# Second products of a dense mixture-of-experts stage turned round: channels on partitions, the gates spread as rows by DMA

## The chip, the core and the metric

The kernel runs on one core of a Trainium2 chip. The metric is device time in microseconds (us) of one execution. Three runs of the kernel before gave 791.85, 794.53 and 795.11 us, a median of 794.53 us. One further execution was recorded by the hardware profiler.

## What is computed

The input is 8 sequences of 256 tokens with 128 channels. The program is a chain of residual blocks: a feed-forward block, an attention block and a feed-forward block with the weights of layer 0, and then the same three of layer 1. The change concerns the two feed-forward blocks of layer 1, here called **f0** (before the attention of layer 1) and **f1** (after it, the last block of the program). Cut to what matters:

```python
def _L1_ffn_ref(x, Wg, W1, W2):           # 2048 tokens, 128 channels, F = 256, E = 8
    probs = softmax(xt @ Wg)
    _, top_idx = top_k(probs.T, T // E)   # every expert takes its 256 best tokens
    masked = where(sel, pT, -inf)
    tok2exp = where(assigned, argmax(masked), argmax(pT))      # one expert per token
    weights = take(probs, tok2exp)
    for e in range(E):
        gate = where(tok2exp == e, weights, 0.0)
        h = gelu(xt @ W1[e]) @ W2[e]
        out = out + gate[:, None] * h
x = x + 0.5 * _L1_ffn_ref(layernorm(x), ...)
x = x + attention(x)
x = x + 0.5 * _L1_ffn_ref(layernorm(x), ...)
```

Which expert a token belongs to is known only when all tokens have been counted for all experts. Each token then needs one expert.

## The kernel before, in words

The tokens lie in 16 tiles of 128. In f0 and f1 the 16 tiles form four groups of four tiles (512 tokens). Two of the groups are **sorted**: their tokens are scattered by expert into a buffer in DRAM (`scattering`, POOL), fetched again as tiles of one expert each (`fetching`, tiles `xs`), turned on PE (`ptpf`), multiplied with the weights of that one expert (`experts`: `phpf`, `pypf`), stored, and gathered back by token (`returning`, POOL, tiles `ygf`). This can begin only after the choice. The other two groups are **dense** (`everyone`): every one of the 8 experts is computed for all their tokens, and what a token doesn't need is multiplied by a gate of zero. This can begin before the choice, and fills PE while the choice is made. Sixteen such units (2 groups by 8 experts) are computed in each block.

A unit of `everyone` has two first products `phf` (line 1652: a 128x128 block of W1 is stationary, the 512 tokens move), two activations `hf` on ACT, and second products `pyf` (line 1670). Before the change a second product keeps 128 tokens of `hf` stationary and moves the 128 columns of W2, so that tokens lie on partitions in the result; a unit has four tiles by two halves of F, eight products. The profile shows every product of 32-bit numbers as two matmul instructions (two passes), so a unit has sixteen `pyf` and four `phf` instructions.

`settling` takes the result. If the gates aren't known yet, ACT copies it out of its bank of PSUM (line 1702: the first eight into `W2`, whose contents are no longer needed, the rest into tiles with the tag `w`). Once the gates are known, DVE adds each of the four tiles with one `scalar_tensor_tensor` (line 1707), with the gate as a value per partition. When eight experts are in, the tile is marked as `moved`. The attention of a sequence waits for both of its tiles; in f0, sequences 0 to 3 lie in the dense groups and 4 to 7 in the sorted ones. The stores of the output wait for the tiles of f1.

The choice (`choosing`) is a search for a threshold in ten rounds. In each round DVE makes candidates and compares (`L1547`, two halves), PE counts with ones (`pcf`, line 1541, eight matmuls a half), and DVE takes the counts and moves the threshold (`L1559`, `L1563`). Then PE ranks ties (`pkf`, line 1575), DVE picks one expert per token, PE counts places (`pcrf`, lines 546 to 571), and DVE computes slots and the gates (line 1620).

No engine chooses its own order. A planner in the kernel (`Weave`) runs all these generators against assumed durations, such as `yield "pe", 1.0, 0.2`, and writes the instructions of each engine down in the order in which its own clock meets them. Each engine then executes its list in that order. A stream of rank -1 (`everyone`) gives way to others that are ready at the same planned time. So an assumed duration decides how many dense products stand between two counts in the list of PE. SP issues the transfers from one list in the same way: the weights of the sorted experts (line 683), the tiles `xs` (line 819), the results of the experts (line 857) and the outputs (line 1750). PSUM has two banks for results of second products (`y`), and a unit that isn't copied holds its bank until DVE has read it.

Of the kernel before, what the change touches and what calls it, by code (L numbers as in the profile page):

```python
# [9 lines left out]
F32 = mybir.dt.float32  # L10
# [3 lines left out]
ALU = mybir.AluOpType  # L14
# [4 lines left out]
P = 128  # L19
B, S, D = 8, 256, 128  # L20
NH, HD = 16, 8
E = 8
SL = P // B
NT = S // SL
TB = 4
# [12 lines left out]
QSCALE = 1.0 / HD**0.5  # L38


LAGS = {"pe": 0.5, "act": 0.3, "dve": 0.2, "pool": 0.2, "sp": 2.5}


# [66 lines left out]
def kernel(ctx: ExitStack, tc: tile.TileContext, a: dict, out: bass.AP):  # L110
# [66 lines left out]
    def bank(tag, k, shape, name):  # L177

        return psum["pool"].tile(shape, F32, tag=f"{tag}{k % BANKS[tag]}", name=name, bufs=1)
# [9 lines left out]
    def woven(dram, moe, pools):  # L189
# [521 lines left out]
        def second1(e, f):  # L711

            cols = slice(F1 + f * D, F1 + (f + 1) * D)
            if isinstance(e, int):
                return l1["W"][:, e, cols]
            return l1["W"][:, bass.ds(e, 1), cols].rearrange("p e d -> p (e d)")
# [786 lines left out]
        def choosing(key):  # L1503
# [125 lines left out]
            c["mine"] = mine  # L1629
            mark(("mine", key))  # L1630

        def everyone(key):

            n_f = F1 // P
            before = None

            yield ("through", unsorted[-1]) if key == "f0" else ("weights of", 4 * B - 1)
            c = chosen[key]
            order = [(k, e) for k in ALL[key] for e in range(E)]
            for n, (k, e) in enumerate(order + [(None, None)]):  # L1640
                hs = []
                if e == 0:
                    yield "head", key, k
                if before:
                    yb = yield from acquire("y")
                    py = bank("y", yb, [P, TB, D], f"py{key}_{n}")
                for f in range(n_f):
                    if k is not None:
                        hb = yield from acquire("h")
                        yield "pe", 1.0, 0.2  # L1650
                        ph = bank("h", hb, [P, BW], f"ph{key}_{n}_{f}")
                        pe.matmul(  # L1652
                            ph, lhsT=l1["W"][:, e, f * P : (f + 1) * P], rhs=c["xT"][k], start=True,
                            stop=True,
                        )
                        h = hidden(f"h{key}_{n}_{f}")

                        def gelu(h=h, ph=ph):
                            act.activation(h, ph, AF.Gelu)  # L1659

                        weave.spawn(emptying(hb, 0.6, gelu, GELU))
                        hs.append((h, hb))
                    if before:

                        for i in range(f * TB // n_f, (f + 1) * TB // n_f):
                            for b in before[1]:
                                yield "free", "h", b
                            yield "pe", 0.5, 0.2
                            for ff in range(n_f):
                                pe.matmul(  # L1670
                                    py[:, i, :], lhsT=before[0][ff][:, i * P : (i + 1) * P],
                                    rhs=second1(before[3], ff), start=ff == 0, stop=ff == n_f - 1,
                                )
                if before:
                    weave.spawn(settling(key, py, yb, before[2], before[3], n), 3 if ("gate", key) in weave.done else None)
                if e == E - 1:
                    mark(("through", (key, k)))
                before = [h for h, _ in hs], [b for _, b in hs], k, e


        SHARED = 12

        added = {}
        kept = dict.fromkeys(("f0", "f1"), 0)

        def settling(key, py, yb, k, e, n):

            c = chosen[key]
            src = py
            waits = ("gate", key) not in weave.done  # L1690
            if waits:
                i = kept[key]
                kept[key] += 1
                if key == "f1" and i >= E:
                    yield "weighed", 4 * B - 1
                yield "act", 0.57, 0.15
                if i < E:

                    src = W2[:, i, :].rearrange("p (t d) -> p t d", d=D)
                else:  # L1700
                    src = one([P, TB, D], f"y{key}_{n}", "w", SHARED)
                act.copy(src, py)
                mark(("free", "y", yb))
            yield "gate", key
            for i, t in enumerate(GROUPS[key][k]):
                yield "dve", 0.28, 0.0
                dve.scalar_tensor_tensor(  # L1707
                    x1[:, t, :], src[:, i, :], c["gate"][:, t, e : e + 1], x1[:, t, :], ALU.mult, ALU.add
                )
            if not waits:  # L1710
                mark(("free", "y", yb))
            added[key, k] = added.get((key, k), 0) + 1
            if added[key, k] == E:
                for t in GROUPS[key][k]:
                    mark(("moved", key, t))

        def returning(key):

# [125 lines left out]
        def scoring():  # L1844
            for n in range(4 * B):
                b, j = divmod(n, 4)
                if j == 0:
                    yield "projected", b
                if n == 0:
                    for t in GROUPS["f0"][ALL["f0"][1]]:  # L1850
                        yield "moved", "f0", t
                if n > 2:
                    yield "weighed", n - 3
                q, k, _, _ = made[b]
                pss = yield from s_banks([([P, 2, S], f"ps{b}_{j}_{g}") for g in range(4)])
                yield "pe", 1.05, 0.2
                for kc in range(2):
                    for g in range(4):
                        rows = slice(32 * g, 32 * g + 32)
                        pe.matmul(  # L1860
                            pss[g][0][:, kc, :], lhsT=k[rows, j, kc * P : (kc + 1) * P],
                            rhs=q[rows, :], start=True, stop=True,
                        )
                ws = [one([P, 2, S], f"w{b}_{j}_{g}", "w", SHARED) for g in range(4)]
                relued[n] = ws
                left = [4]
                for g in range(4):
                    weave.spawn(relu_of(n, g, *pss[g], ws[g], left))
# [50 lines left out]
        def attended(b, sums):  # L1919
# [33 lines left out]
            for qc in range(2):  # L1953
# [17 lines left out]
            [  # L1971
                (1, loading()), (1, fetching()), (1, routing()), (1, tensor()), (2, adds()), (2, combines()),
                (0, scanning()), (3, preparing()), (2, constants()), (2, finishing()), (2, moving()), (1, clearing()),
                (1, opening()), (3, heads("f0")), (-1, everyone("f0")), (1, experts("f0")), (2, returning("f0")),
                (3, projecting()), (1, scoring()), (2, weighing()),
                (3, heads("f1")), (-1, everyone("f1")), (1, experts("f1")), (2, returning("f1")), (1, storing()),
            ]
        )

# [70 lines left out]
```

## Time and profile before

| | |
|---|---|
| three runs | 791.85, 794.53, 795.11 us |
| profiled execution, its own time | 793.47 us |
| its span in the trace | 791.7 us |
| PE busy | 694.4 us (88%) |
| weight loads of PE (beside it) | 568.0 us (72%) |
| DVE busy | 520.2 us (66%) |
| ACT busy | 414.7 us (52%) |
| POOL busy | 214.2 us (27%) |

The stretches that matter, read off the timelines of the engines (us from the start of the span):

| | f0 | f1 |
|---|---|---|
| first dense product on PE | 469.50 | 678.78 |
| first count | 491.95 | 696.57 |
| ranking of ties on PE | 518.46 | 722.53 |
| first scatter on POOL | 529.08 | 733.56 |
| SP begins the weights of the sorted experts | 530.02 | 734.49 |
| SP begins the tiles `xs` | 540.78 | 745.90 |
| first sorted tile turned on PE | 545.08 | 748.98 |
| next stage | attention's first scores 564.64 | first gather on POOL 776.41 |

A line of the timeline gives the start, the time from the first start to the last end of equal instructions merged (xN), the engine, the line of the kernel, the operation, and the tiles out and in. What stands in brackets is idle time of that engine before it and what ended it. Ends of matmuls are modelled, so the distance between starts says more than the duration. Buffer numbers are left out of the names: `f` stands for f0 and f1 alike.

### The profile page before, as it was taken

What the parts mean: (1) busy time and instruction counts of PE and PEld (TensorE: products, weight loads), DVE (VectorE), ACT (ScalarE), POOL (GpSimd) and SP (SyncE); (2) the same over time, 40 slices, a digit from 0 to 9 for tenths busy, and PEclk for the clock granted to TensorE, in tenths of its full rate; (3) what the DMA queues carried; (4) which work ended last, traced back from release to release, by engine and by line L of the source; (5) the groups of instructions that cost most, each with busy time, mean ns of one, the idle gap of its engine ahead of it and who ended that gap; (6) DMA issues with size and microseconds to landing.
All of it is one profiled execution on the core that took longest, in us unless ns stands there. A gap on an engine that the chain in (4) does not pass through costs nothing.

```text
span 791.7 us, 17430 instructions
## 1 busy us (share of the span) xinstructions
PE 694.4 (88%) x5538; PEld 568.0 (72%) x5538; DVE 520.2 (66%) x2946; ACT 414.7 (52%) x1002; POOL 214.2 (27%) x327
## 2 busy tenths in 40 slices
PE   5999999978798659878989998998999999999990
PEld 3889998966596449658979886676756565677690
DVE  2545489788998899889712314768377677475811
ACT  4464866833787417624547545333656656543340
POOL 2234530037114310170351301022144242300403
PEclk9999999985899569958979999999999999999996
DMA  9163876615535265455487200014110000000512
GB/s 333 35 210 91 241 223 173 169 48 180 144 97 117 49 200 161 107 174 150 128 251 223 79 12 28 2 42 136 41 39 1 2 2 1 2 1 1 184 47 77
DMA packets 104570, 83.09 MB, mean 105 GB/s; under 512 B 40544, under 2 KB 83808, under 8 KB 104480
## 3 DMA queue, kind: packets, MB, share of 16 engines
q1 hardware_dynamic: 99568, 71.59, 31.1%
q0 software_dynamic: 4480, 9.18, 3.7%
q10 hardware_dynamic: 432, 1.20, 0.4%
q8 instruction: 46, 0.75, 0.4%
q14 instruction: 44, 0.36, 0.2%
HBM read 57.94 MB, written 24.00 MB: 104 GB/s over the span
## 4 chain that ended last, share of the span: by engine, by line
PE 60%; DVE 24%; DMA 5%; POOL 4%; issue 3%; ACT 3%; SPq 0%; POOLq 0%; ACTq 0%; DVEq 0%
PE phpout L898 6%; PE pypout L875 5%; PE ps L1860 5%; PE pa L1904 4%; PE pyf L1670 3%; PE pmo L1297 3%; PE phdin L769 3%; PE pydin L779 3%; PE phpin L898 2%; PE phf L1652 2%; DVE x L1707 2%; DVE r L1265 2%; DVE mk L1234 2%; PE pypin L875 2%; DVE u L1256 2%
## 5 line engine op out<-in xcount | busy, mean ns | idle before, releaser
L1670 PEld LDWEIGHTS pyf<-w_W,hf 128*128 128x128 f32 x512 | 68.1, 193 | 19.0 <-issue 18.6
L902 ACT ACTIVATE hpout<-phpout,w 128x128 f32<-128x128 f32 x224 | 63.9, 369 | 28.8 <-PE phpout L898 24.2
L1670 PE MATMUL pyf<-w_W,hf 128*128 128x128 f32 x512 | 76.0, 282 | 0.0
L1659 ACT ACTIVATE hf<-phf 128x512 f32<-128x512 f32 x64 | 38.1, 597 | 67.3 <-PE phf L1652 67.2
L1652 PE MATMUL phf<-xTf,w_W 128*128 128x512 f32 x128 | 66.8, 606 | 0.0
L898 PE MATMUL phpout<-xTpout,w 128*128 128x128 f32 x448 | 62.9, 287 | 1.4 <-ACT xTpout L848 1.4
L898 PEld LDWEIGHTS phpout<-xTpout,w 128*128 128x128 f32 x448 | 57.7, 202 | 3.4 <-ACT xTpout L848 2.0
L875 PE MATMUL pypout<-W,hpout 128*128 x448 | 59.7, 277 | 0.0
L1265 DVE SCALAR_TENSOR_TENSOR r<-kbs,dot,e 128x8 f32<-128x8 f32 x251 | 56.2, 224 | 0.0
L1234 DVE TENSOR_TENSOR mk<-Ms,kns 128x72 f32<-128x72 f32 x251 | 55.5, 221 | 0.0
L1256 DVE TENSOR_TENSOR u<-kbs,r 128x64 f32<-128x64 f32 x256 | 55.3, 216 | 0.1
L902 ACT ACTIVATE hpin<-phpin,w 128x128 f32<-128x128 f32 x160 | 45.3, 374 | 19.0 <-PE phpin L898 12.1
L1297 PE MATMUL pmo<-qmo,ident 128*128 128x128 f32 x256 | 43.0, 337 | 14.0 <-DVE qmo L1291 12.5
L875 PEld LDWEIGHTS pypout<-W,hpout 128*128 128x128 f32 x448 | 54.8, 193 | 0.1
L1876 DVE TENSOR_SCALAR w<-ps 128x512 f32<-128x512 f32 x64 | 42.6, 684 | 17.6 <-PE ps L1860 17.0
L1261 DVE TENSOR_TENSOR Ms<-Ms,u 128x64 f32<-128x64 f32 x251 | 53.9, 215 | 0.0
L1229 DVE TENSOR_REDUCE e<-mk 128x8 f32<-128x72 f32 x251 | 53.8, 214 | 0.0
L1297 PEld LDWEIGHTS pmo<-qmo,ident 128*128 128x128 f32 x256 | 40.2, 247 | 16.7 <-DVE qmo L1291 14.4
L1873 ACT ACTIVATE w<-ps 128x512 f32<-128x512 f32 x64 | 36.2, 597 | 25.8 <-PE ps L1860 25.7
L898 PE MATMUL phpin<-xTpin,w 128*128 128x128 f32 x320 | 44.0, 283 | 1.7 <-ACT sps L1049 0.9
L1860 PE MATMUL ps<-q,k 32*128 32x256 f32 x512 | 43.1, 403 | 2.3 <-ACT w L1873 1.3
L898 PEld LDWEIGHTS phpin<-xTpin,w 128*128 128x128 f32 x320 | 40.5, 199 | 3.5 <-ACT sps L1049 1.6
(382 smaller groups left out, 1606.4 us busy)
## 6 DMA issues: line engine op xcount, KB each, us to landing
w<-in_w_dram SPq DMA_DIRECT2D x112, 258.0 KB, 3.4
xs<-rows SPq DMA_DIRECT2D x27, 256.0 KB, 4.2
rows<-x SPq DMA_DIRECT2D x5, 768.0 KB, 5.2
w<-in_w_dram SPq DMA_DIRECT2D x30, 128.0 KB, 2.6
rows<-ypout SPq DMA_DIRECT2D x12, 256.0 KB, 3.4
rows<-ypin SPq DMA_DIRECT2D x9, 256.0 KB, 2.5
W<-in_w_dram SPq DMA_DIRECT2D x8, 256.0 KB, 5.2
w_W<-in_w_dram SPq DMA_DIRECT2D x8, 256.0 KB, 4.1
```

Of the source, the lines that this page charges most:

```text
L875: pe.matmul(py[:, t % TB, :], lhsT=h[:, g, :], rhs=of(e, g), start=g == 0, stop=g == n_f - 1)
L898: pe.matmul(ph[:, f, :], lhsT=first(w, f), rhs=xT[:, t % TB, :], start=True, stop=True)
L902: act.activation(h[:, f, :], ph[:, f, :], AF.Relu, bias=bias(w, f))
L1229: dve.tensor_reduce(e, mk, AX.X, ALU.add)
L1234: dve.tensor_tensor(mk, M(t), bc_mid(kn[:, t + 1], HD), ALU.mult)
L1256: dve.tensor_tensor(u, bc(kb[:, t], HD), bc_mid(r, HD), ALU.mult)
L1261: dve.tensor_tensor(M(t + 1)[:, :, :HD], M(t)[:, :, :HD], u, ALU.add)
L1265: dve.scalar_tensor_tensor(r, kb[:, t], dot, e, ALU.mult, ALU.add)
L1297: pe.matmul(pm, lhsT=ident, rhs=qm[:, :, h, :], start=h == 0, stop=h == HD - 1)
L1652: pe.matmul(ph, lhsT=l1["W"][:, e, f * P : (f + 1) * P], rhs=c["xT"][k], start=True, stop=True,)
L1670: pe.matmul(py[:, i, :], lhsT=before[0][ff][:, i * P : (i + 1) * P], rhs=second1(before[3], ff), start=ff == 0, stop=ff == n_f - 1,)
L1860: pe.matmul(pss[g][0][:, kc, :], lhsT=k[rows, j, kc * P : (kc + 1) * P], rhs=q[rows, :], start=True, stop=True,)
```

## The change

The second product of a dense unit keeps a 128x128 block of W2 stationary and moves 512 tokens of `hf`: two products of 512 columns instead of eight of 128. Channels now lie on partitions, so a gate is no longer a value per partition. The gates of both dense groups are copied (`gs`), turned on PE, copied by ACT (`gT`) and written to DRAM as 16 rows of 512 (`gating`). For each of the 16 units one DMA then reads one row for all 128 partitions into a tile `gb`, of which there are three. DVE multiplies the unit's result with it and adds it to a sum per group (`adding_up`), and at the end PE turns the sum back and DVE adds it to the tokens (`joining`). Thirteen units are copied out of PSUM by ACT; the last three stay there until DVE multiplies them. Tiles of the tag `w` become twelve named tiles, shared with the attention. The planner's price of a dense product of either kind becomes `DENSE`.

```diff
+DENSE = 0.65
...
                 for f in range(n_f):
                     if k is not None:
                         hb = yield from acquire("h")
-                        yield "pe", 1.0, 0.2
+                        yield "pe", DENSE, 0.2
...
-                        for i in range(f * TB // n_f, (f + 1) * TB // n_f):
-                            for b in before[1]:
-                                yield "free", "h", b
-                            yield "pe", 0.5, 0.2
-                            for ff in range(n_f):
-                                pe.matmul(
-                                    py[:, i, :], lhsT=before[0][ff][:, i * P : (i + 1) * P],
-                                    rhs=second1(before[3], ff), start=ff == 0, stop=ff == n_f - 1,
-                                )
+                        yield "free", "h", before[1][f]
+                        yield "pe", DENSE, 0.2
+                        pe.matmul(
+                            py, lhsT=second1(before[3], f), rhs=before[0][f], start=f == 0, stop=f == n_f - 1
+                        )
...
-        def settling(key, py, yb, k, e, n):
...
-            for i, t in enumerate(GROUPS[key][k]):
-                yield "dve", 0.28, 0.0
-                dve.scalar_tensor_tensor(
-                    x1[:, t, :], src[:, i, :], c["gate"][:, t, e : e + 1], x1[:, t, :], ALU.mult, ALU.add
-                )
+        def keeping(key, py, yb, k, e, n):
...
+            if ("ready", key, 0) not in weave.done and i < E + 5:
...
+                src = W2[:, i, :] if i < E else shared(f"y{key}_{n}", i - E)
+                act.copy(src, py)
...
+        def gating(key):
+            yield "gate", key
+            if key == "f1":
+                yield "weighed", 4 * B - 1
...
+            dve.tensor_copy(
+                g.rearrange("p (q e b) -> p q e b", q=2, e=E),
+                chosen[key]["gate"][:, : 2 * TB, :].rearrange(by, q=2),
+            )
...
+            pe.transpose(pt, g, ident)
...
+            act.copy(gT, pt)
...
+            sync.dma_start(out=d.rearrange("r (b t) -> (r b) t", t=P), in_=gT)
...
+            for i in range(2 * E):
+                yield "given", key, i
+                if i > 2:
+                    yield "gated", key, i - 3
...
+                gb = shared(f"gb{key}_{i}", 5 + i % 3)
+                row = ALL[key].index(k) * E + e
+                sync.dma_start(out=gb, in_=d[row : row + 1, :].to_broadcast([P, BW]))
...
+        def adding_up(key, ready):
...
+                dve.tensor_tensor(z, src, gb, ALU.mult)
...
+                if count[k]:
+                    yield "dve", 0.6, 0.0
+                    dve.tensor_tensor(sums[k], sums[k], z, ALU.add)
...
+        def joining(key, k, sums):
...
+            for i in range(TB):
+                pe.transpose(pt[:, i, :], sums[:, i * P : (i + 1) * P], ident)
...
+            dve.tensor_tensor(xs, xs, pt, ALU.add)
...
+            for t in g:
+                mark(("moved", key, t))
```

## The prediction

> **What bounds the kernel now.** I read the list of groups first. One row each for the dense second and first products:
>
> ```profile
> L1670 PE MATMUL pyf<-w_W,hf 128*128 128x128 f32 x512 | 76.0, 282 | 0.0
> L1652 PE MATMUL phf<-xTf,w_W 128*128 128x512 f32 x128 | 66.8, 606 | 0.0
> ```
>
> PE never waits before either (last column 0.0), so whatever waits in PE's weight loads is hidden. Next the timeline of f1, PE. A round of the search, and the distance between starts:
>
> ```profile
> 702.78 1.10 PE L1652 MATMUL phf<-xTf,w_W 128*128 128x512 f32 x2
> 703.73 0.61 PE L1670 MATMUL pyf<-w_W,hf 128*128 128x128 f32 x4
> 704.46 0.37 PE L1541 MATMUL pcf<-x,ones 128*128 128x56 bf16 x8
> 704.67 0.69 PE L1670 MATMUL pyf<-w_W,hf 128*128 128x128 f32 x4
> 705.20 0.37 PE L1541 MATMUL pcf<-x,ones 128*128 128x56 bf16 x8
> 705.40 1.10 PE L1652 MATMUL phf<-xTf,w_W 128*128 128x512 f32 x2
> ...
> 744.91 1.05 PE L1670 MATMUL pyf<-w_W,hf 128*128 128x128 f32 x8
> 745.80 1.02 PE L1652 MATMUL phf<-xTf,w_W 128*128 128x512 f32 x2
> 746.66 0.61 PE L1670 MATMUL pyf<-w_W,hf 128*128 128x128 f32 x4
> 748.98 0.65 PE L844 MATMUL ptpf<-ident,xs 128*128 128x128 f32 x4 [1.71 <-DMA xs<-rows]
> ```
>
> The reader sees: a round takes 2.62 us (702.78 to 705.40). A 512-column product (two passes) takes 0.86 (745.80 to 746.66), or 0.94 after a count (702.78 to 703.73 is 0.95). Eight 128-column passes take 0.89. From the second count to the next first count the search itself needs 1.88 (705.20 to 707.08 by the same view). Then POOL, SP and the end of the expert stage:
>
> ```profile
> 733.56 1.08 POOL L611 DMA_INDIRECT rows<-xnf,slotrf  x1 [41.22 <-DVE pastrf L584]
> ...
> 776.41 0.98 POOL L1738 DMA_INDIRECT ygf<-rows,slotrf  x1 [32.63 <-DMA rows<-ypf]
> ```
> ```profile
> 734.49 9.92 SPq L683 DMA_DIRECT2D w<-in_w_dram  x15
> 745.90 1.48 SPq L819 DMA_DIRECT2D xs<-rows  x3
> ```
>
> So the block's end is a chain: search, scatter, fetch, experts, gather. The dense work is filling. It costs only where it delays that chain or, in f0, the attention, which needs the dense sums too.
>
> **The change, part by part.**
>
> *Second products.* A unit's 16 passes of 128 columns (two times 0.89, 1.78 us) become 4 passes of 512 (two times 0.86, 1.72). 0.06 us a unit, 32 units: 1.9 us of PE. The weight loads that vanish were beside PE. So the change buys almost no PE time.
>
> *Order on PE.* The planner priced a unit at 4.0 us (two of 1.0, four of 0.5); now 2.6 (four of 0.65). The rows say 3.5 and 3.44. Believing dense products cheap, it writes more of them in front of the chain. I counted them in the built order. f1: 18 stand before the last logits (`plf`), 7 more before the first count, then exactly 30 from there to the tie ranking (three a round), then 6 before the place count.
> - Logits: 678.78 + 18 x 0.86 + the short products of attention between them (2.7 us) = 697.0; before 691.73. The residual they wait for is ready by 694, so no slack.
> - First count: 697.0 + 0.85 + 7 x 0.86 + 0.1 = 704.0; before 696.57. DVE's side would be ready at 701 to 703.
> - A round: 0.21 + 0.94 + 0.21 + 0.94 + 0.86 = 3.16; its second part, 2.01, exceeds the search's own 1.88, so PE sets it. Ten rounds: ranking at 735.6, before 722.53: **+13.1**.
> - Ranking 1.45 and six products 5.24 take 6.7, DVE's chain there took 5.66 (722.53 to 728.19); later a product less stands in the way. First scatter **+13.5**.
>
> f0, the same way from 469.50: PE stood 2.98 us waiting for tokens at 479.17, and the extra products fill that; so the first count moves only from 491.95 to 494.0. Ten rounds: ranking 525.6 for 518.46 (+7.1). First scatter **+8.1**.
>
> *Gates on SP.* The gate rows and broadcasts enter SP's list among the weights of the sorted experts: five loads, the gate write, seven loads, three broadcasts, three loads, three broadcasts, then the first `xs`. A load takes 0.66 (9.92/15; f0: 10.44/15 = 0.70). f1: SP starts at 748.0, so broadcast 0 goes at 756.4. Its landing isn't in the trace: 2.0 (the 128 KB outputs) to 4.3 (256 KB `xs` in f0, 540.78 to 545.08); I take 3.4, the 258 KB weight loads, whose form is nearest (2 KB per partition out of DRAM). [...]
>
> Broadcasts 3, 4, 5 wait on SP until DVE has freed the three tiles, and the first `xs` is queued **behind them**. A 128x512 multiply takes 0.67 (L1876 shows 0.684; the 128x512 additions of PSUM 0.54 to 0.67), an addition the same: a pair 1.3. Broadcast 0 lands at 759.8, products 0 to 2 end at 762.4, `xs` goes at 762.9, where the scatter alone allowed 759.4. It reaches PE at 766.0 (3.1 later, as 745.90 to 748.98); before 748.98. f0: broadcast 0 at 546.9, `xs` at 553.4, PE at 557.7; before 545.08.
>
> *Sums.* Per three units: landing 3.4, multiply 0.67, issue 0.1, 4.2 us, 1.4 a unit (DVE alone 1.3). The 128 removed additions cost 22.4 + 12.4 + 7.0 = 41.8 us by their three rows and the 64 new operations 64 x 0.65 = 41.6; nothing is won, but they started 0.1 after the gates and now start 25 us after. PE's list has the turn of group 0 after expert tile 2 and that of group 1 before tile 10, and PE waits at each for its sum. Broadcast 15 stands in SP's list behind the first expert store. The last unit's second product, too, waits for a bank that product 0 frees.
>
> *Experts.* PE idles, but for that unit, from 748 to 766 in f1 (f0: 541 to 557.7). The row for what follows an idle:
>
> ```profile
> 744.00:748.00 4.00, 3.27 (x18) 2.12 (x17) 3.72 (x12) 1.21 (x3) 0.00 (x0) 1.00 0.56 166
> 748.00:752.00 4.00, 3.02 (x13) 1.98 (x14) 3.79 (x13) 0.83 (x2) 0.00 (x0) 0.81 0.78 227
> 752.00:754.00 2.00, 2.00 (x11) 2.00 (x11) 1.40 (x6) 0.74 (x2) 0.00 (x0) 0.52 0.25 73
> ```
>
> (Third number from the end: granted clock.) After 1.71 us idle it fell to half, for 3.4 us; four passes took 0.87 instead of 0.45. After a like 1.88 us in f0 it did not fall. I take half clock for the first 8 groups of four passes, 3.4 us extra in each block. [...]
>
> f1: 766.0 + turn 1.05 + copy 0.8 + 8 x 0.87 = 774.8; group 0's sum is ready at 775.0, so 775.1; three groups to 776.45, store, broadcast 15 at 777.7, landing and pair until 782.4; PE has done 12 groups by 781.9 and waits; turn to 782.95, 11 groups of 0.45 and small stalls: experts end at 788.2; before 773.0. **+15.2**, and the tail of gather and output follows unchanged (18.7 us). Removed from this stretch is 6.3 us of dense work (nine `pyf` rows, two `phf` between 749 and 762); it is in the sum, as the walk contains none.
>
> f0: 557.7 + 1.05 + 0.8 + 6.96 = 566.5; broadcast 15's product ends 573.8, turn to 574.35, ten groups, so attention's first turn is at 578.85. From it to the scores I count turn, copy, product, two copies: 3.2; 582.0. Before:
>
> ```profile
> 556.08 0.46 PE L1806 MATMUL pta<-ident,xna 128*128 128x128 f32 x2
> ...
> 564.64 1.56 PE L1860 MATMUL ps<-q,k 32*128 32x256 f32 x20
> ```
>
> **+17.4** (before, experts were mixed in between). Attention itself loses 2.8 us of expert products still in it after 564.64 and gains about 1.5 at the second sequence, whose root on POOL now stands behind four gathers: -1.3, between -3 and +3.
>
> **Sum**: 17.4 - 1.3 + 15.2 = 31.3. The profiled execution's own time is 793.47 (span 791.7 plus 1.8), 0.13% under the median 794.53: **825 us**.
>
> Bounds: landing 2.0 saves 1.4 at the start of each block and little after (DVE's 1.3 then binds): -3. Landing 4.3 makes 1.7 a unit, +6 a block: +12. No half clock: -6. Attention +-3. Together 812 to 840.
>
> **Rivals.**
> - *Faster, about 784.* The expert stretches lose their dense work: 6.3 us in f1 and 2.7 in f0 (545.57 to 551.5), 9 together. For it: both stretches are full on PE. It decides only if sorted tiles reach PE later by less than these; I have 17.0 and 12.6. At 0.65 a product a round would be 2.6, as now, and most of the delay gone; but the 512-column row shows 0.86. 6%.
> - *Milder, 798 to 812.* The delay is paid once, because dense work done early needn't be done late and the sums come in time: landing 2.0, no half clock, attention absorbing some. Two blocks of about 7 us. 12%.
> - *The broadcasts bind, 840 to 860.* 128 reads of one row are slow, over 5 us, and the ring of three tiles runs at 1.9 a unit: 16 x 0.5 more a block, and `xs` behind it. 7%.
> - *No change.* It does what it says, but the dense work is filling and other waits cover the rest: 790 to 797. 4%.
>
> The forecast, 812 to 840, has 71%. The range reaches into its neighbours: 807 to 843. A run of this kernel can be told from no change at about 0.5%. Faster 0.06, same 0.04, slower 0.90.
>
> **What would show it.** Rounds of 3.1 to 3.2 us; rankings 7 and 13 us later within their block; first `xs` on SP after the sixth broadcast; PE idle over 10 us before the sorted tiles, with half clock after; PE waiting for DVE's sum at both turns. Wrong if a 512-column second product took clearly under 0.86, if broadcasts landed in 2 us, or if the attention hid the shift.

## The result, and the profile after

The changed kernel takes 847.22 us (median of 4 runs, 844.49 to 849.31) against 794.21 (4 runs of the kernel before on the same chip): **1.067 times as long, interval 1.0632 to 1.0709**. The forecast had the sign and the chain, but 825 us is 22 us short, and the range ended at 843.

Everything before f0 is the same program. So I compare from the first dense product of f0 to the end: **322.2 us before, 377.1 after, 54.9 more**. That stretch is cut at the attention's first turn (`pta`) and at the first dense product of f1 (after the change at 468.01, 582.21, 709.91 and the end at 845.06 us of the span):

| us | f0 to `pta` | attention | f1 to the end | sum |
|---|---|---|---|---|
| before | 86.6 | 122.7 | 112.9 | 322.2 |
| after | 114.2 | 127.7 | 135.2 | 377.1 |
| more | 27.6 | 5.0 | 22.3 | 54.9 |

From the profile of the changed kernel, the row of its second products and the row for the reads of the gate rows:

```profile
L1676 PE MATMUL pyf<-hf,w_W 128*128 128x512 f32 x128 | 70.8, 640 | 26.2 <-DVE sumf L1757 26.2
```
```profile
gbf<-gdf SPq DMA_DIRECT2D x32, 256.0 KB, 3.6
```

The second products are busy for 70.8 us where they were for 76.0, but PE now stands 26.2 us in front of them, 13 a block, for DVE's first product with a gate. A gate row lands in 3.6 us by the median (3.1 to 6.2).

The timeline of PE in f1 after the change, one round of the search:

```profile
734.35 0.37 PE L1543 MATMUL pcf<-x,ones 128*128 128x56 bf16 x8
734.56 1.10 PE L1676 MATMUL pyf<-hf,w_W 128*128 128x512 f32 x2
735.50 0.37 PE L1543 MATMUL pcf<-x,ones 128*128 128x56 bf16 x8
735.71 1.10 PE L1662 MATMUL phf<-xTf,w_W 128*128 128x512 f32 x2
736.65 1.02 PE L1676 MATMUL pyf<-hf,w_W 128*128 128x512 f32 x2
737.51 0.37 PE L1543 MATMUL pcf<-x,ones 128*128 128x56 bf16 x8
```

A round is 3.16 us from first count to first count (737.51 less 734.35), as forecast; it was 2.62. No line has a bracket: PE sets the pace with its three dense products. Then SP's queue in f1:

```profile
787.18 1.31 SPq L1743 DMA_DIRECT2D gbf<-gdf  x3
789.40 1.39 SPq L685 DMA_DIRECT2D w<-in_w_dram  x3
792.91 2.41 SPq L1743 DMA_DIRECT2D gbf<-gdf  x3
795.62 0.38 SPq L821 DMA_DIRECT2D xs<-rows  x1
```

Rows 3 to 5 wait for DVE to free their tiles, and the first sorted tile goes behind them, 17.7 us after the first scatter (777.90); before it was 12.3. What this makes of PE shows in the windows of f1 (PE, PEld, DVE, ACT, POOL busy; third from the end the granted clock):

```profile
777.90:799.94 22.04, 4.14 (x5) 1.30 (x5) 6.85 (x15) 0.26 (x1) 7.81 (x8) 0.57 0.66 204
799.94:826.50 26.56, 21.89 (x143) 20.41 (x143) 15.39 (x24) 9.49 (x22) 0.00 (x0) 0.81 0.55 166
```

The same view before, from the first scatter to the first sorted tile:

```profile
733.56:748.98 15.42, 13.71 (x79) 9.70 (x77) 13.91 (x47) 5.37 (x9) 8.09 (x8) 1.00 0.63 195
```

From the first scatter to the first sorted tile PE works 4.1 of 22.0 us, and DVE 6.9; before, in 15.4 us, PE worked 13.7 and DVE 13.9. The sums that DVE did in this wait now come behind it. In f0 the attention needs them. DVE's timeline there (first product with a gate, last pair, addition to the tokens) and PE's:

```profile
549.15 0.69 DVE L1757 TENSOR_TENSOR sumf<-pyf,gbf 128x512 f32<-128x512 f32 x1 [12.29 <-DMA gbf<-gdf]
...
575.35 0.69 DVE L1757 TENSOR_TENSOR zf<-yf,gbf 128x512 f32<-128x512 f32 x1 [1.62 <-DMA gbf<-gdf]
576.08 0.69 DVE L1763 TENSOR_TENSOR sumf<-sumf,zf 128x512 f32<-128x512 f32 x1
```
```profile
567.87 0.87 PE L1774 MATMUL pjf<-ident,sumf 128*128 128x128 f32 x4 [2.37 <-DVE sumf L1763]
...
576.82 0.66 PE L1774 MATMUL pjf<-ident,sumf 128*128 128x128 f32 x4 [0.54 <-DVE sumf L1763]
...
582.21 0.47 PE L1871 MATMUL pta<-ident,xna 128*128 128x128 f32 x2
```

DVE waits 12.3 us for the first row and then needs 26.2 us for 15 units (575.35 less 549.15), **1.75 a unit** where I had 1.4; in f1 it is 1.75 too (26.3 us for 15, from 792.19). The turn of the second sum at 576.82 lets the attention's first turn go at 582.21, 114.2 us after the first dense product; before it was 86.6.

### The profile page after: what moved, and what is told of

The parts are those of the page before. It is cut to its first block, busy times and chain, and to the rows that moved or that the text cites. A ratio compares the mean times of both kernels' runs of the same rounds, so it can differ in the third digit from the quotient of the medians.

```text
span 845.1 us, 16714 instructions
## 1 busy us (share of the span) xinstructions
PE 709.9 (84%) x5172; PEld 545.5 (65%) x5172; DVE 527.6 (62%) x2884; ACT 419.1 (50%) x1009; POOL 212.9 (25%) x327
## 4 chain that ended last, share of the span: by engine, by line
PE 62%; DVE 16%; DMA 10%; POOL 4%; issue 3%; ACT 3%; SPq 2%; POOLq 0%; DVEq 0%; ACTq 0%
PE phf L1662 6%; PE pyf L1676 6%; PE phpout L900 5%; DMA gbf<-gdf 5%; PE pypout L877 5%; PE ps L1925 4%; PE pa L1972 4%; PE pmo L1299 3%; PE phdin L771 3%; PE phpin L900 3%; PE pydin L781 3%; PE pypin L877 2%; PE phdout L771 2%; PE pydout L781 2%; DVE r L1267 2%
## 5 line engine op out<-in xcount | busy, mean ns | idle before, releaser
L1676 PE MATMUL pyf<-hf,w_W 128*128 128x512 f32 x128 | 70.8, 640 | 26.2 <-DVE sumf L1757 26.2
L1299 PE MATMUL pmo<-qmo,ident 128*128 128x128 f32 x256 | 42.7, 336 | 13.9 <-DVE qmo L1293 12.2
L1676 PEld LDWEIGHTS pyf<-hf,w_W 128*128 128x128 f32 x128 | 23.1, 198 | 45.0 <-issue 45.0
L1299 PEld LDWEIGHTS pmo<-qmo,ident 128*128 128x128 f32 x256 | 40.1, 246 | 16.4 <-DVE qmo L1293 13.9
L1925 PE MATMUL ps<-q,k 32*128 32x256 f32 x512 | 46.8, 429 | 3.7 <-ACT q L1893 1.9
L613 POOL DMA_INDIRECT rows<-xnf,slotrf x16 | 15.6, 976 | 108.4 <-DVE pastrf L586 104.1
```

Source lines behind the costliest of these rows:

```text
L1299: pe.matmul(pm, lhsT=ident, rhs=qm[:, :, h, :], start=h == 0, stop=h == HD - 1)
L1676: pe.matmul(py, lhsT=second1(before[3], f), rhs=before[0][f], start=f == 0, stop=f == n_f - 1)
L1925: pe.matmul(pss[g][0][:, kc, :], lhsT=k[rows, j, kc * P : (kc + 1) * P], rhs=q[rows, :], start=True, stop=True,)
```

## Experiments

Two theories at the start. **A**: each block pays by itself, by the order on PE and by the gate rows (they stand before the sorted tiles, and they pace the sums). **C**: the order on PE is nearly all. Others are named where they come. On the chip of e5 to e8 all runs are longer (the kernel before takes 861.25 us, and f0 begins at 525 to 528 us instead of 468 to 473), so those four are read by the stretches from the first dense product. In the search these agree between the chips (first dense product of f1 to the ranking: 56.04 us in every kernel that keeps the changed products and prices). But the kernel before has no trace on that chip, so its 322.2 us are another chip's. By the median times the four lie 47.8, 48.3, 37.7 and 26.8 us above the kernel before, by the stretches 55.7, 59.6, 49.6 and 36.0; for the other runs the two measures differ by at most 4.4. What these four say is therefore uncertain by some 10 us.

| us | f0 to `pta` | attention | f1 to the end | sum | ratio to before, interval |
|---|---|---|---|---|---|
| e1 f1 only | 86.5 | 122.8 | 133.7 | 342.9 | 1.018 to 1.030 |
| e2 f0 only | 114.5 | 128.2 | 112.0 | 354.8 | 1.031 to 1.038 |
| e3 three rows | 106.3 | 127.8 | 132.2 | 366.3 | 1.051 to 1.057 |
| e4 before, cheap | 93.3 | 135.4 | 118.2 | 346.9 | 1.026 to 1.038 |
| e5 rows by POOL | 114.5 | 127.8 | 135.6 | 377.9 | 1.049 to 1.062 |
| e6 PE filled | 114.5 | 130.9 | 136.4 | 381.8 | 1.050 to 1.064 |
| e7 grained | 107.6 | 135.3 | 129.0 | 371.8 | 1.031 to 1.049 |
| e8 turned back | 110.3 | 121.7 | 126.2 | 358.2 | 1.025 to 1.037 |
| e9 rows by PE | 111.8 | 127.7 | 143.4 | 382.9 | 1.074 to 1.086 |
| e10 third later | 114.6 | 124.4 | 135.7 | 374.6 | 1.059 to 1.070 |
| e11 e9 grained | 118.5 | 119.7 | 130.8 | 369.0 | 1.055 to 1.067 |
| e12 before, true | 87.6 | 131.1 | 113.1 | 331.8 | 1.004 to 1.010 |
| e13 no rows | 95.6 | 123.1 | 122.4 | 341.2 | 1.014 to 1.025 |
| e14 no rows, grained | 99.4 | 123.1 | 119.7 | 342.3 | 1.018 to 1.029 |
| e15 before, dear | 95.5 | 121.7 | 115.7 | 332.9 | 1.008 to 1.018 |

**e1 and e2: one block each.**

```diff
+                        if key == TURNED:
+                            pe.matmul(py, lhsT=second1(before[3], f), rhs=before[0][f], ...)
+                        else:
+                            pe.matmul(py4[:, i, :], lhsT=before[0][ff][:, i * P : (i + 1) * P], ...)
```

> Only the last block (f1) has the turned products, the gate rows and the sums; f0 has the products, the copies and the additions of the kernel before. Theory A (each block pays for itself: search delayed by the order on PE, sorted tiles behind the gate rows, sums late): f0 and attention stay as before and f1 is 22 us longer, 794 + 22 = 816 us. Theory B (much of the loss comes from the two blocks acting on each other, through the shared tiles and the attention between them): f1 alone costs under 15 us, below 809.

> Only f0 is turned; f1 is as before. Theory A: f0 loses 22 us up to the first scores of the attention and the attention itself 9, so 825 us; the 9 us of the attention appear here too, because the order of its last sequence on PE changes with f0 alone (the third routing product stands before the last scores). Theory B: the attention is as long as before (114 us from the first scores to the first dense product of f1), 816 us or less.

Measured: 813.18 and 824.67 us (before on that chip 796.49). In e1 only f1 is longer, by 20.8 us; in e2 f0 by 27.9 and the attention by 5.5. Together they make 53.3 of the 54.9. By the medians it is 16.7 and 28.2 us, 44.9 of the 53.0; e1's interval, 14 to 24 us, just reaches B's 15. By the traces the blocks pay separately: theory A, not B.

**e3: three gate rows.**

```diff
-                gb = shared(f"gb{key}_{i}", 5 + i % 3)
+                gb = ready[i - 3][3] if i > 2 else shared(f"gb{key}_{i}", 5 + i % 3)
...
-                sync.dma_start(out=gb, in_=d[row : row + 1, :].to_broadcast([P, BW]))
+                if i < 3:
+                    sync.dma_start(out=gb, in_=d[row : row + 1, :].to_broadcast([P, BW]))
```

> As the changed kernel, but only three of the sixteen gate rows are read in each block and used for all units (the gates of 13 units are wrong; products, sums and turns are unchanged). Theory A (the gate rows on SP hold back the sorted tiles and pace the sums): first sorted tile 4 to 5 us earlier in each block, the sums paced by DVE at 1.35 us a unit, the experts' end about 10 us earlier in each block, 827 us. Theory C (the order on PE is nearly all of the loss, the rows are covered): 842 to 847.

Measured: 837.97 us; the stretch is 10.8 shorter, half of the 20 expected. The tiles come 4.2 and 3.8 us earlier and DVE does a unit in 1.3, both as expected. The time lies between A and C. But the sums still begin at the first row, 12 us after the gates, so the attention's first turn comes 7.9 earlier and no more. The ring of three tiles is the smaller part of what rows cost.

**e4: the kernel before with cheap prices.**

```diff
-                        yield "pe", 1.0, 0.2
+                        yield "pe", 0.65, 0.2
...
-                            yield "pe", 0.5, 0.2
+                            yield "pe", 0.325, 0.2
```

> The kernel before, with only the planner's prices of its dense products lowered in the proportion of the change (0.65 for a first product, 0.325 for each quarter of the second; together 2.6 a unit for 4.0). Products, copies and additions are those of the kernel before, nothing is read from DRAM for gates. Theory A: the search is later by 9 us in f1 and 4 in f0, the attention takes the other order (5 us), and the dense work that is gone from the wait for sorted tiles gives part of it back: 803 to 812 us. Theory C (order is nearly all): 830 or more. Theory D (order costs nothing, it is only moved): 791 to 798.

Measured: 820.80 us, 24.7 more in the stretch: between A and C, so A had the order too small. The search is later by 6.3 and 8.0 us. The rest I put down to the dense work that was spent early: from f0's first scatter to its first sorted tile PE is busy for 6.7 of 14.9 us (before 14.1 of 16.0), and the experts, begun later, run into the attention until 35.7 us after its first turn (before 18.6); the attention takes 12.7 longer. In it, the third routing product of f1 also stands where the changed kernel has it.

**e5: rows from POOL's queue.**

```diff
-                yield "sp", 0.4, 0.0
+                yield "pool", 0.4, 0.0
...
-                sync.dma_start(out=gb, in_=d[row : row + 1, :].to_broadcast([P, BW]))
+                pool.dma_start(out=gb, in_=d[row : row + 1, :].to_broadcast([P, BW]))
```

> As the changed kernel, but the sixteen gate rows of a block are issued by POOL, whose list is empty between the scatters and the gathers, so nothing of them stands before the sorted tiles on SP; three tiles for rows as before, and the planner writes the turn of group 0 some products later. Theory A (rows pace the sums, and the sums end last): the first sorted tile comes 4 to 5 us earlier in each block, but PE then waits for the sum of group 0, and the end of each block comes only 0 to 4 us earlier: 840 to 847 us. Theory E (what hurts is that the tiles stand behind the rows on SP): 5 us in each block and more by the attention, 835 or less.

Measured: the same (377.9), and the tiles did not come earlier, so this doesn't separate A from E. POOL's timeline in f0 shows why:

```profile
598.46 0.96 POOL L613 DMA_INDIRECT rows<-xnf,slotrf  x1 [0.30 <-issue]
602.62 0.61 POOL L1743 DMA_DIRECT2D gbf<-gdf  x1 [3.20 <-issue]
603.53 1.00 POOL L613 DMA_INDIRECT rows<-xnf,slotrf  x1 [0.30 <-issue]
```

The planner put the first row between two scatters, and the scatter behind it waits 3.2 us with it. The rows only changed the list in which they stand in front of the tiles. In f1 the scatters lose less, and the first tile is asked for 15.8 us after the first scatter instead of 17.7; it reaches PE no earlier, and f1 takes 135.6 us for 135.2.

**e6: PE kept busy before the tiles.**

```diff
+        def filling(key, i, hb, n):
+            idle = bank("h", hb, [P, BW], f"idle{key}_{i}")
+            for _ in range(n):
+                pe.matmul(idle, lhsT=l1["W"][:, 0, :P], rhs=chosen[key]["xT"][ALL[key][1]], ...)
```

> As the changed kernel, with 19 more products of 512 columns a block in the time in which PE stands still before the sorted tiles (14 behind the turn of the gates, 5 behind the last second product), whose results nobody reads. Theory A: full clock for the first experts (four passes in 0.45 us instead of 0.87), which brings the third tile forward by 3 to 4 us a block; but PE then waits for the sum of group 0, so that 1 to 3 us a block remain: 841 to 846 us. Theory F (the fallen clock is a main term): 7 us and more, below 840. If the products stand in the way of the tiles: 847 to 852.

Measured: no gain by the stretch, 381.8 (3.2 of the difference in the attention, which the edit doesn't touch, and which I can't explain); by the medians 48.3 us above before, in A's range. PE in f0:

```profile
622.08 0.61 PE L877 MATMUL pypf<-w_W,hpf 128*128 x4
...
626.84 0.66 PE L1786 MATMUL pjf<-ident,sumf 128*128 128x128 f32 x4 [3.26 <-DVE sumf L1775]
```

Four passes take 0.45 from 622.08 on, before the sum and behind it, where the changed kernel needed 0.85 for its first groups and again for three groups behind the sum. But PE now waits 3.26 us for the sum instead of 2.37. The attention's first turn comes at 114.5, as without it. In f0 the fallen clock lies behind the sums and costs nothing. In f1 this is not shown as well: half the clock remains for 6.9 us behind the first tile (changed 10.2), and the tiles come 2.1 and 1.3 us later in the two blocks.

**e7: the old grain.**

```diff
-                        pe.matmul(
-                            py, lhsT=second1(before[3], f), rhs=before[0][f], start=f == 0, stop=f == n_f - 1
-                        )
+                        for i in range(2) if f == n_f - 1 else ():
+                            cols = slice(i * BW // 2, (i + 1) * BW // 2)
+                            for ff in range(n_f):
+                                yield "pe", DENSE / 2, 0.2
+                                pe.matmul(py[:, cols], lhsT=second1(before[3], ff), rhs=before[0][ff][:, cols], ...)
```

with `DENSE` 1.0.

> As the changed kernel, but a second product is cut into two halves of 256 columns, each of its four parts is planned by itself, and the prices are those of the kernel before (1.0 for a first product, 0.5 for a quarter of the second). So the order of dense work and counts is nearly that of the kernel before, while gate rows, sums and turns stay; the planner now puts the turn of group 0 in front of the first expert's second product. Theory A: ranking of ties 6 (f0) and 12 us (f1) earlier, as in the kernel before; the sorted tiles still stand behind the rows, PE waits for the sum of group 0 before nearly all experts (3 us more a block), dense work fills the wait and keeps the clock (3 us less a block): 822 to 832 us. Theory C (order is nearly all): below 805.

Measured: by the ratio at the end of A's range (37.7 us above before), by the stretch 371.8, only 5.3 better. The search is repaired (ranking at 48.6 and 47.4 us; before 49.0 and 43.8; changed 56.1 and 56.0). What it wins is lost to the rows: first scatter to first sorted tile 24.6 and 25.0 us (changed 21.2 and 22.0). The attention takes 135.3; I have no cause for the whole of that.

**e8: turned back unit by unit.**

```diff
-                dve.tensor_tensor(z, src, gb, ALU.mult)
+                for t in range(TB):
+                    pe.transpose(pt[:, t, :], src[:, t * P : (t + 1) * P], ident)
+                for t, tile_no in enumerate(GROUPS[key][k]):
+                    dve.scalar_tensor_tensor(
+                        x1[:, tile_no, :], pt[:, t, :], chosen[key]["gate"][:, tile_no, e : e + 1], ...)
```

> As the changed kernel up to the gates (same products, same prices, same order of the search), but without gate rows and without sums: PE turns every unit's result back by itself (four turns, 0.45 us) and DVE adds it with the gates per partition as in the kernel before. Theory A: the sorted tiles come as soon as scatter and weights allow (5 us earlier in f0, 6 in f1), the additions end about 22 us after the gates instead of 40, the attention gets back its old order (5 us): 816 to 823 us, about what the cheap prices alone cost. Theory C (order is nearly all): 840 or more. Theory G (turning 16 units back on PE is as dear as the rows): 830 to 845.

Measured: 358.2, 18.9 better by the stretch, where 24 to 31 were expected; by the medians 26.8 above before, 26.2 better than the change, which is A's range. PE in f0 shows what stands in the way:

```profile
612.79 1.12 PE L846 MATMUL ptpf<-ident,xs 128*128 128x128 f32 x4 [11.19 <-DMA xs<-rows]
613.70 1.06 PE L1724 MATMUL pjf<-ident,W 128*128 128x128 f32 x4
```

The turn of the eighth unit stands in PE's list behind the sorted tile; PE waits 11.2 us for the tile, and DVE has nothing to add.

**e9: rows spread by PE.**

```diff
-                sync.dma_start(out=gb, in_=d[row : row + 1, :].to_broadcast([P, BW]))
+                for t in range(TB):
+                    r = (ALL[key].index(k) * E + e) * TB + t
+                    pe.matmul(gb[:, t * P : (t + 1) * P], lhsT=ident[:n, r : r + 1].to_broadcast([n, P]), rhs=gT, ...)
```

> As the changed kernel, but a gate row is spread over the partitions by four matmuls with a column of ones (the turned gates stay in SBUF) into a bank of PSUM, instead of being written to DRAM and read back by SP; products, prices, order of the search, sums and turns stay. Measured from the first dense product of f0 to the end the kernel before took 322 us, the changed one 377. Theory A (the way through DRAM and SP's list costs some 20 us): sorted tiles 4 to 6 us earlier in each block, the sums paced by DVE at 1.4 us a unit from 2 us after the gates, 352 to 362 us on this measure, 30 to 40 above the kernel before. Theory C (order is nearly all): 370 or more.

Measured: 855.64 us and 382.9, worse than the change. Theory A failed here: to spread the rows on PE costs as much as the way through DRAM and SP's list. (382.9 lies where C has it, but e13 below rules C out.) SP is free, the tiles are asked for 11.6 us after the first scatter as before the change, and yet:

```profile
551.39 10.60 PE L1739 MATMUL gbf<-gTf,ident 64*128 64x128 f32 x48 [0.89 <-DVE sumf L1761]
561.92 1.11 PE L846 MATMUL ptpf<-ident,xs 128*128 128x128 f32 x4
```

The tile is there, but six rows stand before its turn on PE, each waiting for DVE to free a bank. And the last rows stand behind experts, so the second sum is turned at 577.46, about where it was. In f1 PE's clock comes on top:

```profile
793.50:824.20 30.70, 30.70 (x131) 27.92 (x130) 14.34 (x22) 4.05 (x9) 0.00 (x0) 0.50 0.11 32
```

By the trace PE is busy for all of these 30.7 us, and yet the granted clock is at half throughout; f1 takes 143.4 us for 135.2. So e9 can't say what the way through DRAM costs by itself.

**e10: the third routing product later.**

```diff
+                if (key, k) == ("f1", 2):
+                    yield "weights of", 4 * B - 4
```

> As the changed kernel, but the routing products of the third group of f1 (its turn and its logits) are let into the planner's list only after the last sequence's first scores, as they stood before them in the kernel before. Theory A (their place in PE's list is why the attention takes 5 us more from its first turn to the first dense product of f1): this stretch falls from 127.7 to 122 to 124 us, and the end comes 4 to 6 us earlier. Theory H (the attention is longer because all its first sequences start together, without experts between them): 127 or more.

Measured: the attention takes 124.4 instead of 127.7, with the clock at full in its end (1.00 from 690 to 709 us), just above A's 122 to 124; the stretch is 2.5 less, where A had 4 to 6; the ratio alone (1.0642) could not tell it. What the place costs is told under the attention below.

**e11: e9 and e7 together.** The two edits above in one kernel.

> Both: rows by PE, and the second product in parts of 256 columns at the prices of the kernel before, so that the search keeps its old order. Turned products, sums and turns at the end are what is left of the change. Theory A (order and the way of the gates are the whole loss): first dense product of f0 to the end 328 to 338 us, 6 to 16 above the kernel before. Theory I (the sums themselves, 64 operations of DVE after the gates and the turns behind them, cost much): 345 or more.

Measured: 369.0, far from 338. In f0 the ranking is at 48.5, but the attention's first turn at 118.5: the last rows and the last dense products stand among the experts in PE's list, and DVE waits 9.6 and 6.4 us for two of them. The number is in the range of theory I, but by e13 below the sums themselves are not dear; it is their place, among the experts.

**e12 and e15: other prices in the kernel before.** Edits as in e4, with 0.86 and 0.44, and with 1.15 and 0.575.

> The kernel before with the planner's prices at what the profile shows (0.86 for a first product, 0.44 for a quarter of the second; it has 1.0 and 0.5). Somewhat more dense work stands before the first count of f1 (42 entries for 35). Theory A (the planner's price matters by what it puts in front of the chain): 4 to 8 us later than the kernel before. Theory J (true prices plan better): 1 to 4 us earlier, a kernel that beats both.

> The kernel before with the planner's prices of dense products raised by 15% (1.15 and 0.575). Less dense work stands before the counts (35 entries for 42 in f0, 33 for 35 in f1) and more of it among the experts. Lower prices cost 24 us (at 0.65) and 6 (at 0.86). If it goes on in this direction it is a kernel that beats both: 2 to 5 us earlier. If the old prices are at the bottom: 0 to 6 us later.

Measured: 797.72 for 791.80 us, 1.0069 (1.0036 to 1.0103), and 805.42 for 795.87, 1.0129 (1.0075 to 1.0184). (The profiled execution of e12 took 806.09, 8.4 above the median, so its row in the table is too long.) The first is as theory A had it, the second is worse than expected (0 to 6). The old prices are the best of the four. In e15 PE searches faster (ranking at 47.3), but the attention's first turn comes 8.9 later, since the dense work left over stands among the experts: DVE waits 3.2, 5.9 and 3.5 us for late second products. No version that I ran beats the kernel before.

**e13 and e14: no rows at all**, in the changed order and in the old one.

```diff
-                sync.dma_start(out=gb, in_=d[row : row + 1, :].to_broadcast([P, BW]))
-                ready.append((k, src, yb, gb))
-                mark(("ready", key, i), weave.now + 3.0)
+                ready.append((k, src, yb, l1["W"][:, 0, :]))
+                mark(("ready", key, i))
```

> As the changed kernel, but no gate row is written or read: every unit is multiplied with a block of W1 that lies in SBUF, as soon as the gates are known (the output is that of other gates; products, prices, multiplications, sums and turns stay). Measured from the first dense product of f0 to the end (before 322 us, changed 377, the cheap prices alone 347). Theory A (order 25 us, the rows' way to SBUF the rest): 342 to 352. Theory K (the sums are dear by themselves: 64 operations and two turns that stand in the lists between the gates and the attention): 358 or more.

> As the run before, with the second product in parts of 256 columns and the prices of the kernel before, so that the search has nearly its old order. What is left of the change is the turned product, the sums and the turns. Theory A: 328 to 340 us on the same measure, less than 18 above the kernel before. Theory K: 345 or more.

Measured: e13 takes 811.77 us, 341.2 in the stretch, just below A's range: **without rows 35.9 of the 54.9 us are gone**, 18.6 of them in front of the attention, 4.6 in it, 12.8 in f1. (The planner then also gives the attention back its old order on PE, so the 4.6 are not the rows' own.) DVE in f0:

```profile
537.80 0.68 DVE L1747 TENSOR_TENSOR sumf<-pyf,w_W 128x512 f32<-128x512 f32 x1
...
560.49 0.69 DVE L1767 TENSOR_TENSOR x<-x,pjf 128x512 f32<-128x512 f32 x1 [1.95 <-PE pjf L1764]
```

The first product begins 0.1 us after the gates, and the 16 units are done and added to the tokens 22.7 us later; 14.1 of these lie before the first sorted tile, turned at 551.88. Theory K falls: multiplying and adding is as cheap as the additions of before (23.4 us from the first start to the last end of the sums, 537.80 to 561.18; before 23.0, 529.82 to 552.86), if nothing but the gates is needed for it. The other 19.0 us (9.0 to the attention's first turn, 0.4 in it, 9.5 in f1) I put down to the order; that is not shown, for with the old order of the search e14 comes out no better. It lies between the theories (342.3): its search is the old one, but PE waits for the first sum before the tiles (5.0 us) and DVE for late dense products (3.4, 5.6 and 3.0), which gives back what the search wins.

## Why the prediction was right in kind and short in size

Times from the first dense product of each block, forecast and measured:

| | f0 forecast | f0 | f1 forecast | f1 |
|---|---|---|---|---|
| first count | 24.5 | 24.5 | 25.2 | 24.4 |
| ranking | 56.1 | 56.1 | 56.8 | 56.0 |
| first scatter | 67.7 | 67.8 | 68.3 | 68.0 |
| first sorted tile turned | 88.2 | 89.0 | 87.2 | 90.0 |
| second sum turned | 104.3 | 108.8 | 103.6 | 110.1 |
| attention's first turn; experts' end | 109.4 | 114.2 | 109.4 | 116.6 |
| attention | 116.1 | 127.7 | | |

- **Second products**: right. No gain on PE; what remains of the change is order and gates.
- **Order on PE**: right to a microsecond, down to the round of 3.16 us. The bound "PE sets the round" held.
- **Gates on SP**: right in place (tiles behind row 5). The landing was taken as 3.4; the first row took 5.0 us in f1 (787.18 to 792.19) and 4.7 in f0, while weights were on the way, and the first tile 4.3 behind its issue in f1. That is 2.8 us in f1.
- **Sums**: the term that was mis-sized. "Per three units ... 4.2 us, 1.4 a unit" measured 1.75 a unit in both blocks. With fifteen units that is 5 us a block, and through the turn of the second sum it reaches the attention and the experts' end. The upper bound had 1.7 a unit and 12 us for it. The rival *the broadcasts bind* had 1.9 a unit, 840 to 860 us, and I gave it 7%; its condition, landings over 5 us, did not hold (median 3.6), but the pace lay nearer to it than to mine.
- **Experts at half clock**: the clock fell as forecast (0.61 in the first 10 us of f0's experts), and the walk carried 3.4 us a block for it, the lower bound 6 in all. In f0 e6 shows it hidden: PE waits at the turn for the sum either way.
- **Attention**: the step that failed. "Attention itself loses 2.8 us of expert products ... and gains about 1.5 ...: -1.3, between -3 and +3": from the first scores to the first dense product of f1 I let it fall from 114.1 to 112.8, and it took 123.3; from its first turn to the scores I had 3.2, and it was 4.4. Together I let it shrink from 122.7 (first turn to the first dense product of f1) to 116.1, and it took 127.7, 11.6 more than that. Two things were wrong. First, taking the experts out of it frees PE but not the attention: e14, with the same products on PE in it as the changed kernel and experts only in its first 1.3 us, still takes 123.1. Its own waits fill what is freed: PE is busy in 112.5 of those 123.1 us, before in 117.8 of 122.7 (first before, then e14):

```profile
556.08:678.78 122.70, 117.81 (x1315) 76.37 (x1314) 83.52 (x270) 74.14 (x162) 39.08 (x50) 1.00 0.05 14
```
```profile
567.38:690.49 123.11, 112.53 (x1244) 69.74 (x1243) 85.53 (x271) 70.36 (x152) 41.70 (x54) 0.99 0.03 9
```

  Second, the third routing product of f1 now stands before the last sequence's scores. PE waits there 0.2 and 1.0 us for DVE (e10 has these two as well) and then 0.3 and 0.6 us at the two parts of this product. I counted f1's order on PE but not the attention's. The windows show the clock beside those short waits, first of the changed kernel, then of e14, where PE has the same products and waits in this place:

```profile
690.00:695.00 5.00, 2.90 (x21) 2.12 (x19) 4.16 (x18) 2.94 (x7) 2.18 (x3) 0.95 0.00 0
695.00:700.00 5.00, 4.70 (x26) 3.67 (x26) 2.64 (x14) 0.98 (x3) 1.69 (x2) 0.50 0.01 3
700.00:705.00 5.00, 4.84 (x42) 2.67 (x46) 2.48 (x5) 1.95 (x5) 2.19 (x3) 0.53 0.00 2
```
```profile
675.00:680.00 5.00, 2.88 (x21) 2.13 (x19) 4.17 (x22) 2.58 (x7) 2.17 (x3) 1.00 0.00 0
680.00:685.00 5.00, 4.16 (x57) 2.73 (x56) 4.26 (x14) 2.77 (x6) 2.98 (x4) 1.00 0.00 0
```

  PE is busy for 2.9 of 5 us in both. In the changed kernel the clock is at half for 10.2 us after it, in e14 not. From the turn of that routing product to the first dense product of f1 the seven traces with the fall take 15.9 to 17.1 us (changed 17.0), the two without it 13.1 and 13.2. So 3.8 of the 4.6 us between 127.7 and 123.1 are the fall; the other 7.0 of the 11.6, from 116.1 to 123.1, are what the attention did not shrink.
- **Rivals**: *faster* fell, since tiles came 13.5 and 19.8 us later and not by less than the dense work that left. *Milder* fell: both blocks paid (e1, e2). *No change* fell with the result.

In all, of the 23.5 us that the forecast is short in this stretch, 4.8 lie in f0, 11.6 in the attention and 7.1 in f1.

What stays open: which part of the rows' price is the write and landing and which is only their place in lists, since the other two ways (POOL's queue in e5, PE in e9) put them in front of the tiles again; what the other 19.0 us are; the whole of e7's attention; and why the weight loads of f0 were issued more slowly in three runs on the slower chip, without a wait that the trace shows (13.9 us for 10.4 in e8; 14.7 and 15.5 in e6 and e7, where the changed kernel took 11.6; but 10.5 in e5).

## What to carry to other kernels

Where each engine executes one list in order, ask of a new step not only what it costs but in which list it stands and what is behind it: the additions of before needed only the gates and ran in a wait; the sums need another engine between gates and DVE, and on SP, on POOL and on PE alike that stood in front of the sorted tiles or behind them (35.9 of 54.9 us). A price in a planner is part of the kernel: 35% cheaper prices alone cost 24.7 us with nothing else changed, and the true ones cost 6. And when work is taken out of a stage, look for that stage's own waits before its time is lowered.

## What the runs showed of the hardware

In the attention the granted clock fell after PE had been idle for some 2 us in 5, in pieces of at most 1.0 us, and stayed at half for 10.2 us, worked out from the 0.95, 0.50 and 0.53 of the three windows above (6.8 us in e3). Nine traces have that order and those waits, and in all of them PE is busy for 2.86 to 2.90 of the 5 us: seven show the fall (the changed kernel, e2, e3, e5, e6, e7, e9) and two don't (e4, e14, granted 1.00). No trace shows what decides between the two. In e9 it stayed at half (0.50) for 30.7 us of f1 in which the trace has PE busy for all 30.7; no run shows why.

A gate row of 2 KB read for 128 partitions landed in 3.1 to 6.2 us, not slower by the median (3.6) than the weight loads of 258 KB in the same profile (4.5).
